# Graph layer on one core: sixty-one groups of edges gathered by other engines instead of sixty, first loads issued earlier, and the last node block's steps in another order

## The chip, the core and the metric

The kernel runs on one core of a Trainium2 chip. A core has five engines that each work through their own list of instructions in order: TensorE (PE; its weight loads are listed apart as PEld), VectorE (DVE), ScalarE (ACT), GpSimd (POOL) and SyncE (SP, which here only issues DMAs). They wait for each other and for DMAs through semaphores. The metric is the device time of one execution in microseconds (us); the time of a kernel is the median of its runs.

## The reference

A message-passing layer over 12,500 nodes (128 features each) and 400,000 edges (32 features each), edges sorted by destination:

```python
h = jnp.maximum(_layernorm(x), 0.0)
m = relu(concat([h[src], h[dst], edge_attr]) @ w1 + b1) @ w2 + b2      # per edge
agg = segment_sum(m, dst)                                               # per node
gi, gh = agg @ w_ih + b_ih, h @ w_hh + b_hh                             # a GRU cell
r, z = sigmoid(i_r + h_r), sigmoid(i_z + h_z)
n = tanh(i_n + r * h_n)
out = x + (1 - z) * n + z * h
```

So each edge needs one row that depends on its source (anywhere in the table), one that depends on its destination (close to that of its neighbours in the list), and its own 32 features.

## The kernel before, in words

**Preamble.** x is read in batches (`load`), normalised, transposed into `hT_all` (features on partitions, all nodes in SBUF), and multiplied by the source part of w1 (table A, in DRAM, stored by the DMAs at line 482) and by the destination part (table B). A loop over `q` holds it; each step of `q` takes four tiles of 128 nodes. The stores of A read a tile `asb` that has two buffers, which ACT fills (line 458). The first nine groups below are gathered from x itself while A is not yet there.

**Groups and units.** The 3,125 tiles of 128 edges make 391 groups `k` of 8 tiles (the first has 5). Half a group is a unit `u`, 782 in all. For each group the program does, in this order along the units: load L (destination numbers and edge features of two groups, `fetch`, lines 566 to 577); load RW, two windows of 32 rows of B (`window_rows`, line 613); turn the destination numbers into a one-hot matrix on DVE (`onehot_T`, line 586); multiply both on PE into PSUM (`pre`, line 683); add the source's rows and clamp at zero (`add` on DVE, line 713); sum by destination on PE with a second one-hot matrix (`seg`, line 739); copy the sums out for every second group (`take`, line 748). In the loop `pre` runs three units ahead of `seg`, `add` two units ahead.

**Where the source's rows come from.** Three ways, fixed before the program is built by the table `mode`:
- by POOL: eight indirect DMAs for a group (line 163), into a ring of `GBUFS` = 11 group buffers. POOL may run ahead of the rest by as many POOL groups as the ring holds.
- by hand on ACT (28 groups) or on DVE (27 groups): the engine copies one column of `hT_all` for each edge into a tile `HE_act` or `HE_dve`, 1,024 small copies for a group on ACT (line 979), 512 double ones on DVE (line 986). PE then multiplies the columns by w1a into the same PSUM tile (line 694) and ACT clamps instead of DVE (line 725).
- by hand on SP (5 groups): one DMA per edge.

The copies of a group by hand are spread evenly over the units since the engine's group before (`jobs`, `run_jobs`), and must be done four units before the group's own. Groups by hand are thus spread over the list: the last ones of ACT, DVE and SP are 388, 386 and 379, and ACT's groups lie 14 or 13 groups apart, which gives its jobs 28 or 26 units each.

**Nodes.** When the groups of a block of nodes are done, `node` runs the GRU cell for that block, one step per unit, on PE, DVE and ACT. The last block (groups 382 to 390) has its own routine, `last_node`, whose steps are called at the units listed in `LAST_STEPS`; what is left of it runs after the loop.

**DMA order.** SP issues nearly all DMAs in program order. The DMAs that are not by hand use eight completion counters by turns (DMAHW0 to DMAHW7 in the rows below); an issue waits until the last DMA of its counter has landed.

Of the kernel before, what the change touches and what calls it, by code (L numbers as in the profile page):

```python
# [9 lines left out]
F32 = mybir.dt.float32  # L10
F16 = mybir.dt.float16
I32 = mybir.dt.int32
U8 = mybir.dt.uint8
# [11 lines left out]
PAIR = 2 * GRP  # L25
# [31 lines left out]
START = {"dve": 14, "act": 4, "sp": 24}  # L57
NR = 12672

H_AT = 16512  # L60
# [3 lines left out]
def tile_gnn(ctx: ExitStack, tc: tile.TileContext, x, src, srcT, dstT, dstP, eaT, eaP, w1, b1, w2T, b2,  # L64
# [126 lines left out]
    base_d = at[96:97, :NP - 1]  # L191
    by_hand = [k for m in ("sp", "act", "dve") for k in order[m]]
    NJ = len(by_hand)
# [109 lines left out]
    def setup(pool):  # L303
# [46 lines left out]
        place(0)  # L350

    st_all = const.tile([128, NT, 2], F32, name="st_all")
    nc.vector.memset(st_all[:, NFULL, :], 0.0)
    with tc.tile_pool(name="pp", bufs=3) as pp:
# [85 lines left out]
        for q in range(NC + 3):  # L440
# [36 lines left out]
            if q in (7, 9, 11):  # L477
                batch_store(q // 2 - 3)
            if q >= 3:
                b, i0, c, e, P, n0 = chunk(q - 3)  # L480
                if e == bats[b][1]:
                    nc.sync.dma_start(nodes(A, i0, e, P), asb[b][:P, :e, :])
# [80 lines left out]

    Ls, OH, RT, HE, SEG = ({} for _ in range(5))
    hand = {}

    def fetch(q):
        if q * QP >= NP:
            return
        n = min(QP, NP - q * QP)  # L570
        c = slice(q * QP * 512, (q * QP + n) * 512)
        Ls[q] = p3.tile([128, QP * 512], F32, name="L")
        p = dstP[:, c]
        nc.sync.dma_start(
            Ls[q].bitcast(I32)[:2 * V, :n * 512],
            bass.AP(tensor=p.tensor, offset=p.offset, ap=[list(p.ap[0]), [0, V], [1, n * 512]]))
        nc.sync.dma_start(Ls[q][2 * V:, :n * 512], eaP[:, c])

# [12 lines left out]

    bases = {}

    def block(k):
        return max(b for b in range(NB) if BLOCKS[b][0] <= k)

    def slot(b, i):
        return i // 2 if b < NB - 1 else (BP - BLOCKS[b][1]) // 2 + i // 2

    def window_rows(k):  # L600
        if k >= NP:
            return
        b = block(k)
        k0, n, _ = BLOCKS[b]
        if k == k0:
            _, vals = nc.values_load_multi_w_load_instructions(
                base_i[0:1, b, 0:n], engines=[ET.SP], min_val=0, max_val=4 * D * LAST,
                skip_runtime_bounds_check_because="clamped above")
            for i, v in enumerate(vals):
                bases[k + i] = v  # L610
        v = bases.pop(k)
        for a in range(2):
            nc.sync.dma_start(RW[k % 4].bitcast(U8)[V * a:V * (a + 1), a, :],
                              B_bytes[bass.ds(v + 4 * D * SHIFT * a, 4 * D * V)].rearrange(
                                  "(p f) -> p f", p=V))

# [144 lines left out]
    def zero(p):  # L761
        nc.tensor.matmul(p, zrow[:, :128], zrow[:, :p.shape[1]], start=True, stop=False)
# [94 lines left out]
    def last_node():  # L857
# [36 lines left out]
        yield  # L894
        ph = gate(two[:, 1, :w], 3, True)
        yield
        for i in (n - 3, n - 2):
# [51 lines left out]
    def one_by_one(m, k):  # L949
        et = {"act": ET.Activation, "dve": ET.DVE, "sp": ET.SP}[m]  # L950
        r = by_hand.index(k)
        if m == "sp":
            goal[k] = tc.alloc_semaphore(f"brought{r}"), 16 * PAIR * 128
            G[k] = pj.tile([128, GRP, 2, D], F32, name="G_sp", bufs=1)
            rows = G[k].bitcast(U8)
        else:
            hand[k] = pj.tile([128, PAIR * 128], F32, name=f"HE_{m}")
# [49 lines left out]
    def run_jobs(u, phase):  # L1007
        if phase == 0:
            for m, k, span in jobs.get(u, ()):
                live[m] = [one_by_one(m, k), u, span, PAIR * 128 // STEP[m], 0]  # L1010
# [20 lines left out]

    gathers(0)
    dst_tile(1)
    for q in range(3):
        fetch(q)
    for k in range(4):
        window_rows(k)

# [33 lines left out]
    last = last_node()  # L1072
    LAST_STEPS = (NU - 8, NU - 6, NU - 5, NU - 4, NU - 3, NU - 2, NU - 1)

# [214 lines left out]
```

## Time and profile before

| | us |
|---|---|
| median of 3 runs (range) | 3378.95 (3376.49 to 3381.35) |
| the profiled execution, as timed | 3383.87 |
| its span, first to last instruction | 3382.1 |
| mean granted TensorE clock | 0.795 |
| busy: PE / DVE / ACT / POOL | 2400.4 / 2213.6 / 3081.1 / 2542.8 |

Busy time leaves out instructions that only load registers or issue DMAs, so an engine can be taken up for longer than it is busy; the page's part on groups of instructions shows such time as idle time that "issue" ended. All times below are us from the start of the span, unless said otherwise. A row of the timeline gives start, length, engine, line, operation, output and input, count, and in brackets the engine's idle time before it and what ended that.

### The profile page before, as it was taken

The numbers are of one execution on the slowest core, as the hardware profiler recorded it, in microseconds if no ns is written. First come the engines' busy times: TensorE is split into PE (matmuls) and PEld (weight loads), VectorE is DVE, ScalarE is ACT, GpSimd is POOL, SyncE is SP. The second block draws the span as 40 slices with busy tenths as digits, with TensorE's granted clock in tenths as the row PEclk, the third lists the DMA queues.
The fourth block names the chain that finished last, engine by engine and source line by source line (L and its number), as shares of the span: only waits on it lengthen the run. The fifth ranks groups of instructions, "written<-read, shape, count | busy, mean of one in ns | idle before, by whom it ended". The sixth has DMA issues, their size and how long they took to land. (4 is left out here: it accounts for less than half of the span.)

```text
span 3382.1 us, 93395 instructions
## 1 busy us (share of the span) xinstructions
PE 2400.4 (71%) x13113; PEld 1554.8 (46%) x13113; DVE 2213.6 (65%) x16274; ACT 3081.1 (91%) x29057; POOL 2542.8 (75%) x2654
## 2 busy tenths in 40 slices
PE   7567766776677677668776777677667767766767
PEld 6444444444444444445444444444444444444445
DVE  8566666766666666666667766666656666666665
ACT  7599899999999998998999999999889998988975
POOL 7777777777777777777777777777777777777775
PEclk9778777887888777877877878787777787778778
DMA  6433444444444444444444444444444444343332
GB/s 215 104 92 84 95 99 101 99 97 103 96 95 99 97 98 95 99 104 97 96 98 97 98 95 105 97 99 98 95 98 96 100 95 99 94 96 94 92 94 67
DMA packets 196737, 335.77 MB, mean 99 GB/s; under 512 B 69445, under 2 KB 118148, under 8 KB 196112
## 3 DMA queue, kind: packets, MB, share of 16 engines
q0 software_dynamic: 84640, 173.51, 23.0%
q1 hardware_dynamic: 111327, 156.18, 17.8%
q14 instruction: 517, 4.23, 0.4%
q8 instruction: 109, 1.79, 0.2%
q10 hardware_dynamic: 144, 0.07, 0.0%
HBM read 309.25 MB, written 20.24 MB: 97 GB/s over the span
## 5 line engine op out<-in xcount | busy, mean ns | idle before, releaser
L163 POOL DMA_INDIRECT G<-A,src_i x2576 | 2475.8, 961 | 790.4 <-issue 761.2
L979 ACT COPY HE_act<-hT_all 128x4 uint8 x28672 | 2889.0, 189 | 52.9 <-issue 29.1
L986 DVE SCALAR_TENSOR_TENSOR both<-hT_all 128x4 uint16 x13824 | 1174.3, 154 | 930.3 <-issue 925.6
L683 PE MATMUL pre<-RW,L 128*128 128x256 f32 x3128 | 1136.1, 489 | 461.3 <-DMA RW<-B 237.7
L683 PEld LDWEIGHTS pre<-RW,L 128*128 128x128 f32 x3128 | 662.8, 237 | 736.8 <-issue 420.2
L739 PE MATMUL seg<-RB,OH 128*32 128x129 f32 x6250 | 592.7, 319 | 244.2 <-DVE RB L713 211.9
L739 PEld LDWEIGHTS seg<-RB,OH 128*32 128x32 f32 x6250 | 328.0, 123 | 590.7 <-DVE RB L713 310.1
L713 DVE CUSTOM_DVE_ANT_0 RB<-pre,G 128x1024 f32<-128x1024 f32 x323 | 391.1, 1211 | 70.9 <-DMA G<-A,src_i 56.5
L586 DVE TENSOR_SCALAR L<-L,node_of 64x512 f32<-64x512 int32 x382 | 185.9, 487 | 62.2 <-DMA L<-in_dstP 59.9
L725 ACT ACTIVATE RB<-pre 128x1024 f32<-128x1024 f32 x64 | 65.0, 1016 | 91.0 <-PE pre L694 91.0
L633 DVE TENSOR_TENSOR OH<-dloc,seg 128x512 f32<-128x512 f16 (+1 forms) x198 | 132.3, 669 | 0.0
L765 PE MATMUL nd<-spot,sums 128*128 128x40 f32 x782 | 119.6, 326 | 3.6 <-DVE sums L748 3.6
L765 PEld LDWEIGHTS nd<-spot,sums 128*128 128x128 f32 x782 | 115.5, 237 | 12.7 <-issue 8.8
L991 DVE COPY HE_dve<-both 128x512 uint8<-128x512 uint8 x216 | 97.6, 452 | 7.4
L244 PE MATMUL nd<-w1b,hT_all 128*128 128x128 f32 x224 | 49.4, 368 | 73.1 <-DVE xb L850 73.1
L734 PE MATMUL seg<-zrow 1*128 1x129 bf16 x196 | 45.5, 232 | 78.1 <-DVE OH L633 78.0
L694 PEld LDWEIGHTS pre<-w1a,HE_dve 128*128 128x128 f32 x432 | 89.1, 255 | 12.4
L694 PEld LDWEIGHTS pre<-w1a,HE_act 128*128 128x128 f32 x448 | 85.9, 238 | 11.0
L694 PE MATMUL pre<-w1a,HE_dve 128*128 128x128 f32 x432 | 85.4, 333 | 0.0
L694 PE MATMUL pre<-w1a,HE_act 128*128 128x128 f32 x448 | 83.7, 319 | 0.0
L163 POOL DMA_INDIRECT G<-in_x,src_i x69 | 65.6, 950 | 21.9 <-issue 20.7
L244 PEld LDWEIGHTS nd<-w1b,hT_all 128*128 128x128 f32 x224 | 35.2, 231 | 85.5 <-DVE xb L850 80.0
(177 smaller groups left out, 1346.2 us busy)
## 6 DMA issues: line engine op xcount, KB each, us to landing
G_sp<-A SPq DMA_DIRECT2D x5120, 0.5 KB
L<-in_dstP SPq DMA_DIRECT2D x195, 256.0 KB
L<-in_eaP SPq DMA_DIRECT2D x195, 256.0 KB
G<-A,src_i POOLq DMA_INDIRECT x2576, 2.5
RW<-B SPq DMA_DIRECT2D x782, 16.0 KB
xb<-in_x SPq DMA_DIRECT2D x26, 256.0 KB
out<-xb SPq DMA_DIRECT2D x26, 256.0 KB
xs<-in_x SPq DMA_DIRECT2D x11, 512.0 KB
```

What stands on the lines that cost most here:

```text
L163: fetched = nc.gpsimd.indirect_dma_start(out=G[k][:, j, a, :], out_offset=None, in_=table, in_offset=bass.IndirectOffsetOnAxis(ap=src_i[c] ...
L244: nc.tensor.matmul(pm[:m, i:i + D], hT_all[:, n0 + i:n0 + i + m], w1b, start=True, stop=True)
L586: nc.vector.tensor_scalar(o, i, node_of[:, k:k + 1], None, op0=ALU.is_equal)
L633: nc.vector.tensor_tensor(p, dloc[:, e0:e1, None].to_broadcast(shape), row[:, None, :].to_broadcast(shape), op=ALU.is_equal)
L683: nc.tensor.matmul(p[:, 2 * i:2 * i + 2, :], Ls[k // QP][:, c0:c0 + 128], RW[k % 4], start=True, stop=not raw)
L694: nc.tensor.matmul(p[:, 2 * i + a, :], cols, w1a, start=False, stop=n + 1 == len(l) or l[n + 1][1] != j)
L713: made = nc.vector._custom_dve(TENSOR_ADD_SAT, out=o, in0=p, in1=G[k].rearrange("p j a f -> p (j a) f")[:, c, :], s0=float("inf"), s1=0.0)
L739: nc.tensor.matmul(p[r0:r0 + V, :D + 1], OH[k][:, a * GRP + j, :], RB[k % 2][:, 2 * j + a, :D + 1], start=False, stop=all(b != a for _, _, ...
L765: nc.tensor.matmul(p[:, bass.ds(offs[i], V + SHIFT)], sums[:, slot(b, i), :D], spot[:, i % 2, :], start=False, stop=i == len(offs) - 1)
L979: nc.scalar.copy(he[:, e * 4:e * 4 + 4], column(v))
L986: nc.vector.scalar_tensor_tensor(both[:, (e0 % PIECE + i) // 2, :], column(vals[i + 1]), 256.0, column(vals[i]), op0=ALU.mult, op1=ALU.add)
L991: nc.vector.tensor_copy(he[:, p0 * 4:(p0 + PIECE) * 4].rearrange("p (n c b) -> p n c b", c=2, b=4), both.bitcast(U8).rearrange("p n (b c) ...
```

## The change

Four things are done.

1. The table `mode` is made anew. Group 385 (`SHARED`) is now by hand as well, the 61st: ACT copies its edges 0 to 767 and DVE 768 to 1023, into one `HE_dve` tile. POOL's list is shorter by that group. The other groups by hand keep their numbers (28, 27, 5) but are placed so that ACT and DVE end at group 385 and SP at 371. ACT's last group of its own is 375, DVE's 381. ACT's groups are now 13 apart in 18 of 27 cases (26 units), 14 in 8 and 12 in one.
2. The first L (`fetch(0)`) is issued at q = 4 of the preamble, over ScalarE's queue instead of SP's, into an `HE_dve` buffer that no one uses yet.
3. The RW rows of groups 0 to 3 are issued at q = 16 of the preamble instead of after the first three L.
4. In `last_node` the degrees start one unit earlier (`LAST_STEPS` now holds NU - 7 too), so each gate comes one unit earlier, and the first six sums of the block, which stood beside the degrees, come in a step of their own behind the gates.

```diff
+SHARED, CUT = NP - 6, 768
...
-    mode, order = {}, {m: [] for m in SPREAD}
+    def share(m, k):
+        return (0, PAIR * 128) if k != SHARED else (0, CUT) if m == "act" else (CUT, PAIR * 128)
+
+    mode, order = {SHARED: "both"}, {m: [] for m in SPREAD}
     for m, n in SPREAD.items():
-        lo, hi = START[m] // 2 + 2, NP - {"dve": 5, "act": 3, "sp": 12}[m]
+        lo, hi = START[m] // 2 + 2, NP - 20
+        part = 0
+        if m != "sp":
+            hi, part = SHARED, (share(m, SHARED)[1] - share(m, SHARED)[0]) / (PAIR * 128)
         for i in range(n):
-            k = lo + int((i + 1) * (hi - lo) / n)
+            k = lo + int((i + 1) * (hi - lo) / (n + part))
...
+        order[m] += [SHARED] if part else []
...
+        if q == 0:
+            Ls[q] = pj.tile([128, QP * 512], F32, name="HE_dve")
+        else:
+            Ls[q] = p3.tile([128, QP * 512], F32, name="L")
         p = dstP[:, c]
+        queue = nc.scalar if q == 0 else nc.sync
...
+            if q == 16:
+                for k in range(4):
+                    window_rows(k)
+            if q == 4:
+                fetch(0)
...
-        pt = ps1.tile([128, 512], F32, name="nd")[:, :w]
-        zero(pt)
-        for i in range(n - 3):
-            sum_of(b, pt, offs, i)
         yield
         carry(b, DEG[0:1, :], pd[0:1, :], d)
...
         ph = gate(two[:, 1, :w], 3, True)
+        yield
+        pt = ps1.tile([128, 512], F32, name="nd")[:, :w]
+        zero(pt)
+        for i in range(n - 3):
+            sum_of(b, pt, offs, i)
...
-        for e0 in range(0, PAIR * 128, LOAD[m]):
+        for e0 in range(*share(m, k), LOAD[m]):
...
+    for q in (1, 2):
+        fetch(q)
     dst_tile(1)
-    for q in range(3):
-        fetch(q)
-    for k in range(4):
-        window_rows(k)
...
-    LAST_STEPS = (NU - 8, NU - 6, NU - 5, NU - 4, NU - 3, NU - 2, NU - 1)
+    LAST_STEPS = tuple(range(NU - 8, NU))
```

How the instructions stand now, at three places. A row is line, operation, output and input, size; the brackets name the counters that it waits for (DMAHW0 to 7 of DMAs, the others of engines). Line numbers of the change are higher by 20 to 48 for the same statement.

ACT's list early in the preamble (seg is a PSUM tile with transposed rows, xs the batch of x), before:

```order
L468 COPY hT_all<-seg_79 128x4x128 [waits PE_49]
L458 COPY asb<-pre 128x512 [waits PE_49]
L263 ACTIVATE xs<-xs,st_all 128x128 [waits DMAHW5_49,DVE_49]
L263 ACTIVATE xs<-xs,st_all 128x128 x3
L458 COPY asb<-pre 128x512 [waits DMAHW5_49,PE_49,Activation_49]
```

and with the change, up to the copy that takes the second `asb` buffer again:

```order
L516 COPY hT_all<-seg_79 128x4x128 [waits PE_49]
L373 DMA HE_dve<-in_dstP 64x1x1024 [waits DMAHW7_49]
L376 DMA HE_dve<-in_eaP 64x1024 [waits DMAHW1_49]
L506 COPY asb<-pre 128x512 [waits PE_49]
L271 ACTIVATE xs<-xs,st_all 128x128 x3
L506 COPY asb<-pre 128x512 [waits DMAHW5_49,PE_49,Activation_49]
L271 ACTIVATE xs<-xs,st_all 128x128 x4
L226 ACTIVATE s<-mv,eps 128x8 [waits DVE_49]
L506 COPY asb<-pre 128x512 [waits DMAHW7_49,PE_49,Activation_49]
```

Two DMA issues stand in ACT's list now, and they use the counters DMAHW7 and DMAHW1; the last copy into `asb` waits for the counter DMAHW7.

SP's list at the same time, the second store of A, before:

```order
L375 DMA xs<-in_x 128x1024 [waits DMAHW1_49,PE_49]
L423 DMA at<-in_src 1x1024 [waits DMAHW2_49]
L423 DMA at<-in_src 1x1024 [waits DMAHW3_49]
L423 DMA at<-in_src 1x1024 [waits DMAHW4_49]
L482 DMA A<-asb 128x1024 [waits DMAHW5_49,Activation_49]
```

and with the change:

```order
L423 DMA xs<-in_x 128x1024 [waits DMAHW3_49,PE_49]
L471 DMA at<-in_src 1x1024 [waits DMAHW4_49]
L471 DMA at<-in_src 1x1024 [waits DMAHW5_49]
L471 DMA at<-in_src 1x1024 [waits DMAHW6_49]
L535 DMA A<-asb 128x1024 [waits DMAHW7_49,Activation_49]
L471 DMA at<-in_src 1x1024 [waits DMAHW0_49]
L471 DMA at<-in_src 1x1024 [waits DMAHW1_49]
```

The second store of A now has the counter whose last DMA is the first half of the early L.

PE's list at the end (seg rows are units 779, 780 and 781; pre<-DEG,brow begins a gate; nd<-spot,sums are sums), before:

```order
L739 MATMUL seg_79<-RB_180,OH_185 32x129 x4
L881 MATMUL pre<-DEG,brow 128x320
L884 MATMUL pre<-hT_all,whh_s 128x320
L734 MATMUL seg_80<-zrow 128x129
L739 MATMUL seg_80<-RB_179,OH_183 32x129 x4
L881 MATMUL pre<-DEG,brow 128x320
L884 MATMUL pre<-hT_all,whh_s 128x320
L739 MATMUL seg_80<-RB_179,OH_183 32x129 x4
L765 MATMUL nd<-spot,sums 128x40
```

and with the change:

```order
L758 MATMUL seg_79<-RB_180,OH_185 32x129 x4
L896 MATMUL pre<-DEG,brow 128x320
L899 MATMUL pre<-hT_all,whh_s 128x320
L753 MATMUL seg_80<-zrow 128x129
L758 MATMUL seg_80<-RB_179,OH_183 32x129 x4
L781 MATMUL nd<-zrow 128x320
L784 MATMUL nd<-spot,sums 128x40
L758 MATMUL seg_80<-RB_179,OH_183 32x129 x4
```

Between the last two units' sums by destination there was a gate; now the first six sums of the block stand there (shown by their first two rows).

More of the change, by code (lines that the diff above doesn't have):

```diff
@@ L350, in setup, with fetch, block, window_rows @@
         place(0)
+    Ls = {}
+    def fetch(q):
+        if q * QP >= NP:
+            return
+        n = min(QP, NP - q * QP)
+        c = slice(q * QP * 512, (q * QP + n) * 512)
+        if q == 0:
+            Ls[q] = pj.tile([128, QP * 512], F32, name="HE_dve")
+        else:
+            Ls[q] = p3.tile([128, QP * 512], F32, name="L")
+        p = dstP[:, c]
+        queue = nc.scalar if q == 0 else nc.sync
+        queue.dma_start(
+            Ls[q].bitcast(I32)[:2 * V, :n * 512],
+            bass.AP(tensor=p.tensor, offset=p.offset, ap=[list(p.ap[0]), [0, V], [1, n * 512]]))
+        queue.dma_start(Ls[q][2 * V:, :n * 512], eaP[:, c])
+    bases = {}
+    def block(k):
+        return max(b for b in range(NB) if BLOCKS[b][0] <= k)
+    def window_rows(k):
+        if k >= NP:
+            return
+        b = block(k)
+        k0, n, _ = BLOCKS[b]
+        if k == k0:
+            _, vals = nc.values_load_multi_w_load_instructions(
+                base_i[0:1, b, 0:n], engines=[ET.SP], min_val=0, max_val=4 * D * LAST,
+                skip_runtime_bounds_check_because="clamped above")
+            for i, v in enumerate(vals):
+                bases[k + i] = v
+        v = bases.pop(k)
+        for a in range(2):
+            nc.sync.dma_start(RW[k % 4].bitcast(U8)[V * a:V * (a + 1), a, :],
+                              B_bytes[bass.ds(v + 4 * D * SHIFT * a, 4 * D * V)].rearrange(
+                                  "(p f) -> p f", p=V))
     st_all = const.tile([128, NT, 2], F32, name="st_all")
@@ L561, in check_windows @@
         nc.vector.tensor_copy(flag, f[:, 6:7])
-    Ls, OH, RT, HE, SEG = ({} for _ in range(5))
+    OH, RT, HE, SEG = ({} for _ in range(4))
     hand = {}
[L567 to L577, printed above, removed]
     def onehot_T(k):
```

27 lines of the change are left out of this document (5 added, 22 removed).

## The prediction

> **What bounds the kernel now.** I read the page's busy times and groups first, then the gathers (line 163) and the additions (line 713) counted over stretches from the start, then the timeline of both ends, then the by-hand copies of ACT (line 979) job by job.
>
> ```profile
> PE 2400.4 (71%) x13113; PEld 1554.8 (46%) x13113; DVE 2213.6 (65%) x16274; ACT 3081.1 (91%) x29057; POOL 2542.8 (75%) x2654
> L163 POOL DMA_INDIRECT G<-A,src_i x2576 | 2475.8, 961 | 790.4 <-issue 761.2
> L979 ACT COPY HE_act<-hT_all 128x4 uint8 x28672 | 2889.0, 189 | 52.9 <-issue 29.1
> ```
>
> ACT is the busiest by the page. But POOL's gathers with the idle time ahead of each fill 2475.8 + 790.4 = 3266.2 us, and 761.2 of the idle time is "issue": no one else holds POOL up. One gather costs 3266.2 / 2576 = 1.268 us. Whether POOL or the rest ends last is told by their distance. Line 163 from 0 to 300, 2300 and 3300 us (stretch, busy time and count, clock, DMA share, GB/s), then line 713 in the same stretches:
>
> ```profile
> 0.00:300.00 300.00, 221.02 (x233) 0.84 0.47 128
> 0.00:2300.00 2300.00, 1739.77 (x1811) 0.80 0.42 102
> 0.00:3300.00 3300.00, 2498.89 (x2601) 0.79 0.42 100
> ```
>
> ```profile
> 0.00:300.00 300.00, 12.13 (x10) 0.84 0.47 128
> 0.00:2300.00 2300.00, 265.75 (x219) 0.80 0.42 102
> 0.00:3300.00 3300.00, 387.37 (x319) 0.79 0.42 100
> ```
>
> A group is eight gathers (the first five), so POOL has gathered (233 - 5) / 8 + 1 = 29.5 groups at 300 us, 226.8 at 2300, 325.5 at 3300. Consumed are the additions, plus nine groups from x that need none, less those of SP's groups (0, 3, 4): 19, 225, 324. POOL leads by 10.5 groups, then 1.8, then 1.5: the consumers start far behind, are faster, and have caught up by 2300. From there POOL sets the pace, and its last gather sets the end:
>
> ```profile
> 3344.34 1.02 ACT L725 ACTIVATE RB<-pre 128x1024 f32<-128x1024 f32 x1
> 3344.98 0.95 POOL L163 DMA_INDIRECT G<-A,src_i  x1 [0.30 <-issue]
> 3354.97 0.94 POOL L163 DMA_INDIRECT G<-A,src_i  x1 [0.30 <-issue]
> DMA to landing us min/median/max: 2.5/2.5/2.5
> 3356.16 1.22 DVE L713 CUSTOM_DVE_ANT_0 RB<-pre,G 128x1024 f32<-128x1024 f32 x1 [1.50 <-PE pre L683]
> 3356.87 1.53 PE L765 MATMUL nd<-spot,sums 128*128 128x40 f32 x12
> 3361.10 1.29 DVE L713 CUSTOM_DVE_ANT_0 RB<-pre,G 128x512 f32<-128x512 f32 x2 [3.15 <-PE pre L683]
> 3365.12 0.63 PE L739 MATMUL seg<-RB,OH 128*32 128x129 f32 x8
> 3365.69 0.80 PE L881 MATMUL pre<-DEG,brow 34*128 34x320 f32 x2
> 3367.16 0.63 PE L739 MATMUL seg<-RB,OH 128*32 128x129 f32 x8
> ```
>
> The last gather lands at 3354.97 + 2.5 = 3357.5, and the span ends at 3382.1: a tail of 24.6. A part of it is a late consumer: group 389 landed at 3344.98 + 2.5 = 3347.5 and was added at 3356.16, 8.7 later; group 390 was added 3.6 after landing, behind PE.
>
> **Group 385 leaves POOL.** Eight gathers by 1.268: -10.1 us. Both ends: 9.99 between the last gathers of groups 389 and 390, so eight cost 10.0 to 10.1.
>
> **The first loads.** The start, by the timeline:
>
> ```profile
> 90.21 0.66 SPq L574 DMA_DIRECT2D L<-in_dstP  x1
> 92.84 0.94 POOL L163 DMA_INDIRECT G<-A,src_i  x1 [3.18 <-DMA L<-in_dstP]
> 100.32 0.48 DVE L586 TENSOR_SCALAR L<-L,node_of 64x512 f32<-64x512 int32 x1 [9.76 <-DMA L<-in_dstP]
> 106.01 0.66 PE L666 MATMUL misc<-ident,G 128*128 128x128 f32 x2 [13.77 <-ACT G L263]
> 118.39 1.19 PE L683 MATMUL pre<-RW,L 128*128 128x256 f32 x2 [11.73 <-DMA RW<-B]
> 124.86 0.94 POOL L163 DMA_INDIRECT G<-A,src_i  x1 [2.34 <-PE misc L666]
> ```
>
> The first product waited 9.76 us for L and then 11.73 for RW. With both loads early, both waits go: 21.5 us sooner. By itself this is worth nothing at the end, because POOL, not the consumers, is last there; it is margin for ACT (below). But one wait of POOL goes with it: at 124.86 it stood 2.34 us instead of 0.30 for the transposes at line 666, which now come well ahead. -2.0 us.
>
> **What the early L costs.** It takes DMA counters in the middle of A's stores, and the second store of A now waits until the early L has landed.
>
> ```profile
> 20.00:30.00 10.00, 9.40 (x50) 8.87 (x48) 7.76 (x40) 9.15 (x22) 7.57 (x9) 1.00 0.83 263
> 25.51 0.63 ACT L458 COPY asb<-pre 128x512 f32<-128x512 f32 x1
> 26.56 0.37 SPq L482 DMA_DIRECT2D A<-asb  x1
> 33.95 0.59 ACT L458 COPY asb<-pre 128x512 f32<-128x512 f32 x1 [0.26 <-ACT xs L263]
> 86.31 3.37 SPq L482 DMA_DIRECT2D A<-asb  x3
> ```
>
> Bounds: if L lands before SP comes to that store, nothing. At most it takes as long as later, 90.21 to its use at 100.32, 10.1 us: issued at about 25.7 it lands by 35.8, and the store leaves then and not at 26.56. A store took some 3.4 us (the last three, issued from 86.31 on, let POOL go at 92.84, 89.68 + 3.2), so ACT's copy at 33.95, which needs that buffer back, would start at 39.3, 5.4 late, and SP's next loads stand behind the store as well. Every engine is 76 to 94% taken in that stretch, so little is made up, and A is finished later by 0 to 6 us. I take +4, nearer the upper end, because L is 512 KB in a stretch in which the DMA engines are already 83% taken. POOL's first gather from A comes at 96.8 then, and everything behind it 4 us later. The Trainium skill ("DMA: Bandwidth & Descriptors", "Issuing engines are not separate DMA queues") says that transfers issued by several engines share the same 16 DMA engines, so that a second issuer saves issue time only. It speaks against this part, and by it alone the early L would put off the rest by its bytes, an estimate of 0.524 MB / 263 GB/s = 2.0 us; the term would be +2.0 and the time 2 us shorter. No run here shows the two apart. The RW rows are 8 small DMAs of SP at q = 16; they lie beside the same stores and I cost them at nothing of their own (0 to 2 us if SP's stores are late through them, in the range).
>
> The last gather lands at 3357.5 - 10.1 - 2.0 + 4 = 3349.4.
>
> **The end.** By hand, ACT now ends four units ahead of group 385, at unit 766, and groups 386 to 390 all come from POOL, at 10 us each. At the end of before ACT still copied for group 388, and its clamp at 3344.34 was followed by the last addition of 390 at 3361.10, nine units later: 16.8 / 9 = 1.87 us per unit once the copies are gone, against 5 that POOL takes. So the consumers wait for POOL at the last groups. From the landing, the first of 390's additions (0.65, half of 1.29) and the hand-over (0.15) lead to the sum by destination of unit 780 at 3350.2, where before it was at 3365.12; the rest was 3382.1 - 3365.12 = 17.0. In it six first sums with their zeroing (0.23 + 1.53) now stand where a gate stood (3365.69 to 3367.16, 1.47): +0.3. The last gate stays behind unit 781. 3350.2 + 17.0 + 0.3 = **3367.5**, or -14.6 against 3382.1. The profiled execution took 3383.87, 4.92 more than the median, and the difference is taken over to that: 3378.95 - 14.6 = 3364.
>
> **Whether ACT keeps up.** This is the step on which the sum hangs: ACT gets 0.75 groups more, and its jobs mostly 26 units instead of 28. A job (1,024 copies; line 979 from its first copy to the next job's first: stretch, ACT's busy time and count) does not depend on its units, but on what it waits for:
>
> ```profile
> 142.60:263.80 121.20, 102.34 (x1025) 0.77 0.38 91
> 489.20:602.30 113.10, 102.73 (x1026) 0.79 0.42 99
> ...
> sum 558.80, ACT 515.35; mean ACT 103.07
> ```
>
> ```profile
> 602.30:710.50 108.20, 102.36 (x1024) 0.82 0.42 98
> ...
> sum 655.50, ACT 618.02; mean ACT 103.00
> ```
>
> ```profile
> 710.50:823.80 113.30, 102.39 (x1025) 0.80 0.42 98
> ...
> sum 804.50, ACT 720.22; mean ACT 102.89
> ```
>
> The first row is the first job. Up to 2300, where ACT is not held by POOL, the five jobs of 26 units took 558.8 / 5 = 111.8 us, the six of 28 units right behind them 109.25, the seven later ones 114.9. With 28 units ACT runs ahead and waits for the others; behind a 26 it has fallen back and hardly waits. Now 18 jobs have 26 units and no two of 28 follow each other, so I expect 109.25 for most, and at the worst (8 x 109.25 + 19 x 111.8) / 27 = 111.0. The first job starts 142.6 - 17.5 (21.5 less the 4) = 125.1 and ends 121.2 later, at 246.3; 27.75 jobs more end at 3278 to 3327; twelve units by 1.87 bring the last addition to 3300 to 3349. The landing at 3349.4 is later than either, so POOL still ends last, at the worst by nothing. A price per job of 111.0 is thus the point from which ACT decides. DVE (27.25 groups for 27) and SP (its 5 groups ending sooner) get only 1 to 2% more per unit, against 5% for ACT; should DVE decide instead, that is the same rival (B) by another engine.
>
> **Rivals.** (A) The consumers stay late at the end, so that the tail keeps its 24.6: 3349.4 + 24.6 = 3374.0, median 3371. For it: 389 was 8.7 us behind. Against it: POOL needs 50 us for five groups that cost the consumers 19. Chance 0.13. (B) The other side: ACT becomes the bound. Its place is the jobs of 26 units: if they go on costing the mean of the 18 jobs, (558.8 + 655.5 + 804.5) / 18 = 112.2, then 246.3 + 27.75 x 112.2 = 3360, the last addition at 3382, and some 18 behind it 3400: median 3397, +18. For it: the margin is thin and ACT is 91% busy. Against it: the jobs behind a 26. Chance 0.20. (C) The preamble loses the whole gain: SP's list, which also feeds x, stalls behind the store twice over, 10 us and more instead of 4: the span becomes 3367.5 + 6 to 8 = 3373.5 to 3375.5, the median 3370 to 3372. For it: the 83% of the DMA engines. Against it: the trace has only one store that meets the early L. Chance 0.09.
>
> **How the numbers follow.** The forecast has the remaining 0.58. A measurement of this kernel can tell about 0.2%, 6.8 us, from no change: faster lies below 3372.2, slower above 3385.7. The forecast's own range is 3357 (L costs nothing, and 3 us less of tail) to 3371. Faster: nearly all of the 0.58, most of (A), and what of (C) lies below the bound: 0.68. Slower is (B) but for its mild form just past the point: 0.19. Within: 0.13. The range for eight in ten goes up to 3388, which holds A, C and a mild B.
>
> **What would show it.** POOL issues 2568 gathers from A, the first at about 96 and the last near 3347; no stop of 2.3 us near 125; ACT's copy into `asb` at 34 waits for a DMA (if not, the +4 is wrong); the first clamp of ACT at 109 instead of 126.86 as in this row of before:
>
> ```profile
> 126.86 1.00 ACT L725 ACTIVATE RB<-pre 128x1024 f32<-128x1024 f32 x1
> ```
>
> Line 979's jobs at 109 to 111 us; the additions of 389 and 390 within 4 us of landing. If the additions still trail POOL by two groups at 2300 us and later, with ACT's copies up to unit 766 ending after 3330, (B) holds and the forecast is wrong.

## The result, and the profile after

The changed kernel takes 3391.64 us (median of 8 runs, 3385.58 to 3395.3), the kernel before 3380.59 (8 runs beside them): a ratio of 1.0033, with a 95% interval of 1.0023 to 1.0043. It is slower by 11 us, where 3364 was forecast. The profiled execution of the change took 3386.99, its span is 3385.1 us, 3.0 longer than that of before.

POOL did what it was to do. The last two of its rows and, from the same timeline, the last addition on DVE:

```profile
3340.23 0.94 POOL L171 DMA_INDIRECT G<-A,src_i  x1 [0.30 <-issue]
3341.47 0.94 POOL L171 DMA_INDIRECT G<-A,src_i  x1 [0.31 <-issue]
...
3363.15 1.29 DVE L732 CUSTOM_DVE_ANT_0 RB<-pre,G 128x512 f32<-128x512 f32 x2 [3.46 <-PE pre L702]
```

POOL's last gather starts at 3341.47 instead of 3354.97, 13.5 us sooner. But it lands at about 3344, and the last addition comes 19 us behind that; in before it was 3.6. The consumers, not POOL, now set the end. The gathers (line 171) and the additions (line 732) of the change, counted from 0 to 300, 2300 and 3300 us, in the form in which they were shown of before:

```profile
0.00:300.00 300.00, 216.98 (x228) 0.83 0.47 129
0.00:2300.00 2300.00, 1733.82 (x1812) 0.80 0.42 101
0.00:3300.00 3300.00, 2492.25 (x2603) 0.80 0.42 100
```

```profile
0.00:300.00 300.00, 13.42 (x12) 0.83 0.47 129
0.00:2300.00 2300.00, 260.55 (x215) 0.80 0.42 101
0.00:3300.00 3300.00, 384.19 (x317) 0.80 0.42 100
```

By the same working POOL has gathered 28.9, 226.9 and 325.8 groups, and the consumers have used 12 + 9 = 21, 215 + 9 - 3 = 221 and 317 + 9 - 5 = 321. The lead is 7.9 groups at 300 us (before 10.5, the earlier start is seen in it), but still 5.9 at 2300 (before 1.8) and 4.8 at 3300 (before 2.5: five of SP's groups had been added by then, the last at 3289, not the four of the prediction). The consumers never catch POOL up. By the counts of PE's products of line 702 (683 in before; 8 for a group) between 300 and 2000 us, before and then the change:

```profile
300.00:2000.00 1700.00, 599.70 (x1652) 0.80 0.42 98
```

```profile
300.00:2000.00 1700.00, 594.58 (x1632) 0.80 0.42 97
```

206.5 groups have become 204.0; a group takes 8.33 us instead of 8.23. The page and the start of the change:

```profile
L171 POOL DMA_INDIRECT G<-A,src_i x2568 | 2459.0, 958 | 793.8 <-issue 766.5
...
L702 PE MATMUL pre<-RW,L 128*128 128x256 f32 x3112 | 1140.2, 493 | 447.1 <-DMA RW<-B 288.5
```

```profile
22.80 1.15 ACTq L373 DMA_DIRECT2D HE_dve<-in_dstP  x1
...
36.35 0.37 SPq L535 DMA_DIRECT2D A<-asb  x1
...
39.64 0.58 ACT L506 COPY asb<-pre 128x512 f32<-128x512 f32 x1 [6.02 <-DMA A<-asb]
...
100.46 0.94 POOL L171 DMA_INDIRECT G<-A,src_i  x1 [10.83 <-DMA L<-in_dstP]
...
114.22 1.00 ACT L744 ACTIVATE RB<-pre 128x1024 f32<-128x1024 f32 x1
```

The early L held back the second store of A until 36.35 (26.56 before), ACT's copy waited 6.02 us behind it, and POOL's first gather from A came at 100.46 instead of 92.84: 7.6 us late. Not all of that is the early L's, as the section on the prediction shows. The first clamp came at 114.22 instead of 126.86, 12.6 sooner, where 109 had been forecast.

### The profile page after: what moved, and what is told of

The parts are those of the page before. It is cut to its first block, busy times and chain, and to the rows that moved or that the text cites. A ratio compares the mean times of both kernels' runs of the same rounds, so it can differ in the third digit from the quotient of the medians.

```text
span 3385.1 us, 94355 instructions
## 1 busy us (share of the span) xinstructions
PE 2399.5 (71%) x13129; PEld 1538.9 (45%) x13129; DVE 2221.3 (66%) x16403; ACT 3165.9 (94%) x29826; POOL 2526.0 (75%) x2646
## 5 line engine op out<-in xcount | busy, mean ns | idle before, releaser
L171 POOL DMA_INDIRECT G<-A,src_i x2568 | 2459.0, 958 | 793.8 <-issue 766.5
L784 PE MATMUL nd<-spot,sums 128*128 128x40 f32 x782 | 104.3, 301 | 1.3 <-DVE sums L767 1.3
L784 PEld LDWEIGHTS nd<-spot,sums 128*128 128x128 f32 x782 | 100.3, 210 | 9.2 <-issue 7.5
L833 PE MATMUL nd<-DEG,brow 34*128 34x512 f32 (+2 forms) x112 | 69.8, 706 | 29.8 <-ACT gt L843 29.5
L713 PEld LDWEIGHTS pre<-w1a,HE_dve 128*128 128x128 f32 x448 | 78.7, 219 | 9.3
L1000 ACT COPY HE_dve<-hT_all 128x4 uint8 x768 | 77.1, 189 | 1.5 <-issue 0.8
L713 PE MATMUL pre<-w1a,HE_dve 128*128 128x128 f32 x448 | 76.9, 300 | 0.0
```

What stands on the lines that cost most here:

```text
L171: fetched = nc.gpsimd.indirect_dma_start(out=G[k][:, j, a, :], out_offset=None, in_=table, in_offset=bass.IndirectOffsetOnAxis(ap=src_i[c] ...
L713: nc.tensor.matmul(p[:, 2 * i + a, :], cols, w1a, start=False, stop=n + 1 == len(l) or l[n + 1][1] != j)
L784: nc.tensor.matmul(p[:, bass.ds(offs[i], V + SHIFT)], sums[:, slot(b, i), :D], spot[:, i % 2, :], start=False, stop=i == len(offs) - 1)
L833: nc.tensor.matmul(pg, brow[:, c], DEG[:, :w], start=True, stop=False)
L1000: nc.scalar.copy(he[:, e * 4:e * 4 + 4], column(v))
```

## The experiments

Four theories were tried. **T**: the consumers set the end, and of them ACT's copies alone set the pace. **R1**: POOL still sets the end, and its late start on A ate the gain. **T2**: ACT and DVE together set the pace. **T3**: SP sets it, because the rows of B (RW), which PE needs for each product, stand on SP's queue behind the row loads of SP's own groups. Each ratio is to the kernel before, run beside the version. There before takes 3379.3 to 3382.5 us, but about 5700 beside six of the runs, which the last part of this section is about.

**Which parts cost or bring something: e1b, e3b, f1, f2.** e1b has the table of before, e3b the first L on SP behind the preamble, f1 and f2 are one kernel with both.

```diff
e1b, f1, f2:
-    mode, order = {SHARED: "both"}, {m: [] for m in SPREAD}
+    mode, order = {}, {m: [] for m in SPREAD}
-        lo, hi = START[m] // 2 + 2, NP - 20
+        lo, hi, part = START[m] // 2 + 2, NP - {"dve": 5, "act": 3, "sp": 12}[m], 0
e3b, f1, f2:
-            if q == 4:
-                fetch(0)
...
-    for q in (1, 2):
+    for q in range(3):
         fetch(q)
```

> The table of before (60 groups) with the early first L, the early rows of B and the last block's new order; again, on a chip on which before takes about 3380. Theory T: the consumers catch POOL up before 2400 and POOL, which starts on A 7.6 us later, sets the end: 3380.6 + 7.6 - 2 - up to 3 = 3383 to 3386. Rival R1 (POOL sets the end in the change too): 3391.6 + 10 = 3402.

Measured: 3385.56 us, 1.0019 (1.001 to 1.0028), as T had it; R1's 3402 is out.

> The first L back on SP behind the preamble, all else as in the change; again, on a chip on which before takes about 3380. POOL's first gather from A at 92 to 94 instead of 100.5. Theory T (consumers set the end): as the change or up to 3 us more, 3391 to 3394. Rival R1 (POOL sets the end): 7.6 us less, 3384.

Measured: 3392.7 us, 1.0041 (1.0027 to 1.0054), the time of the change, though POOL starts on A at 95 instead of 100.5. So POOL's start does not set the end of the change; R1 falls. The consumers' start does not show in the time either: PE's first product comes at 118.39 in before, at 111.00 in e3b and at 105.39 in the change, 7.4 us sooner by the early rows of B and 5.6 more by the early L.

> The table of before (60 groups by hand), the first L on SP behind the preamble as before, the early rows of B and the last block's new order kept: the change without its 61st group and without its early L. Theory T: POOL sets the end as in before; its first gather from A is at 92 to 94 again, the wait of 2 us near 125 is gone, and the consumers start 11 us sooner: 2 us faster than before, 3376 to 3381 on a chip on which before takes 3380.6. Rival R1 (POOL's start alone counts): 3378 too. Rival R2 (the consumers' pace sets the end in before as well): 11 us faster, 3370.

> The version without the 61st group and the early L (table of before, early rows of B, new order of the last block), now timed. All theories: POOL sets the end; the wait of 2 us near 125 is gone, so 1 to 3 us faster than before, 3376 to 3379; if the last block's new order is worth anything it shows here as more than that.

Measured: f1 3381.53 beside 3382.47 (one run each), f2 3379.97, 0.9997 (0.9988 to 1.0006). Without the 61st group and the early L the change is worth nothing that can be measured; the 1 to 3 us expected of f2 do not show. e1b and f2 differ by the early L: e1b is 6.2 us above its before, f2 0.6 below its own, 6.8 apart. POOL's first gather from A is at 100.42 in e1b and at 94.09 in f2, 6.3 apart. Where POOL sets the end, the early L is a loss of that size.

**ACT or DVE: e2b, g1, h1, h2.** e2b gives DVE 256 of ACT's edges of the shared group; h1 lets DVE load 16 column numbers at a time. g1 is e2b and e3b together, h2 is g1 and h1.

```diff
e2b, g1, h2:
-SHARED, CUT = NP - 6, 768
+SHARED, CUT = NP - 6, 512
h1, h2:
-LOAD = {"act": 16, "dve": 32, "sp": 32}
+LOAD = {"act": 16, "dve": 16, "sp": 32}
```

> Group 385 cut in half between ACT and DVE (ACT 512 of its edges instead of 768), all else as in the change; again, on a chip on which before takes about 3380. Theory T (ACT's copies set the consumers' pace, and the consumers the end): 256 copies fewer on ACT, 27 us, so the consumers end up to 27 us sooner, down to where POOL's landing at 3345 and a tail of 20 set the end: 3365 to 3375. Rival R2 (DVE sets the pace): a quarter of a group more on DVE, 28 us: 3405 to 3420. Rival R1 (POOL): no change, 3391.

> A version put together from the parts: 61 groups with group 385 cut in half, the first L back on SP behind the preamble, early rows of B, the new order of the last block. Theory T: POOL's last gather lands at about 3345 - 7.6 = 3338, the consumers' last addition comes where e2b has it; the later one and 20 us of tail set the end: 3362 to 3372, the same as e2b where the consumers decide. Rival R2 (DVE sets the pace): 3405 to 3420. Rival R1: 3384.

Measured: e2b 3400.07, 1.0051 (1.0037 to 1.0065); g1 3398.85, 1.0051 (1.0037 to 1.0064). By the medians they are 8 and 7 us slower than the change; the intervals overlap with its own, so that this much is not certain, but they are not faster by 20. ACT's 27 whole jobs, of 1,024 copies in both, took 112.7 us each in e2b, where its groups lie a little farther apart, and 110.8 in the change. So it is not the number of its copies that sets ACT's pace, and T in this form falls; but R2's 28 us are not there either. The places moved by more than the one group that was expected (ACT's last own group from 375 to 379, DVE's from 381 to 378), and both shares of group 385 end late, ACT's at 3348.9 and DVE's at 3348.0, against 3327.9 and 3330.4 in the change:

```profile
3317.82 31.08 ACT L1000 COPY HE_dve<-hT_all 128x4 uint8 x307
...
3347.57 0.43 DVE L1012 COPY HE_dve<-both 128x512 uint8<-128x512 uint8 x1
```

The clamp of group 385 cannot come before that. What makes the shares late, and whether it is all of the 8 us, was not tried.

> The change with DVE loading its column numbers 16 at a time instead of 32; the copies and all else stay. In the change DVE stands 955 us ahead of its copies with 'issue' as the reason, 1.1 us for each of 872 loads of 32; a load of 32 takes 2.15 us on its queue, one of ACT's 16 takes 1.05. Theory T2 (ACT and DVE share the blame: each waits for the other, and both are full): the standing time falls by a third or more, DVE comes free, ACT's full jobs go from 110.8 to 108 or 109, the consumers end 40 us or more sooner, POOL's landing at 3345 sets the end: 3366 to 3378. Theory T (ACT alone): ACT's jobs stay at 110 to 111, no change, 3388 to 3394. If loads of 16 hide no better than those of 32, DVE stands longer, 2 x 1 us for 32: the jobs get longer and the time goes up by 20 or more, which again speaks for DVE as part of the bound.

> As the run before with loads of 16, and group 385 cut in half (ACT 512), and the first L back on SP behind the preamble. If loads of 16 help, theory T2: both engines end sooner, POOL lands at 3339 and sets the end: 3358 to 3368. Theory T: ACT is relieved by 27 us, DVE no matter: 3365 to 3375. If loads of 16 hurt: 3410 or more.

Measured: h1 3383.76, 1.0022 (1.0012 to 1.0032); h2 3386.18, 1.0024 (1.0011 to 1.0037). The row of DVE's copies in h1:

```profile
L1007 DVE SCALAR_TENSOR_TENSOR both<-hT_all 128x4 uint16 x13952 | 1227.8, 156 | 862.8 <-issue 848.3 <-DMA RW<-B 2.1 <-DMA L<-in_eaP 1.6
```

DVE stood 863 us instead of 955, a tenth less and not a third, so the run was a weak test. The groups went no faster: between 300 and 2000 us they were 203.0 against 204.0, and the last addition came at 3361.6 against 3363.15. Both times lie between the ranges that were given. By the median h1 is 8 us faster than the change, by the ratios 4, and the intervals overlap. That DVE has no part is not shown by it; i2 below is the stronger test.

**One engine at a time: i1, i2, i3.** Each leaves out a quarter of one engine's by-hand work in its own groups; for ACT:

```diff
+        if m == "act" and k != SHARED:
+            return 0, 768
         return (0, PAIR * 128) if k != SHARED else (0, CUT) if m == "act" else (CUT, PAIR * 128)
...
+        if m == "act" and k != SHARED:
+            nc.scalar.copy(hand[k][:, 768:1024], hT_all[:, 0:256])
         for e0 in range(*share(m, k), LOAD[m]):
```

> The change, but in each of ACT's 28 own groups only 768 of 1024 columns are copied one by one; the last 256 come as one block of wrong columns, so part of the sum is wrong. ACT loses a quarter of its work, some 25 us a job; places and all else stay. Theory T (ACT alone sets the consumers' pace, 8.35 us a group between groups 30 and 230): the pace falls to where the next engine stands, 7.9 or less, the consumers catch POOL up, and POOL's landing at 3345 with a tail of 20 sets the end: 3364 to 3372. Theory T2 (ACT and DVE, each waiting for the other): the pace falls to 8.1 or 8.2 only, the end is still POOL's: 3364 to 3375. Theory T3 (ACT and SP, whose row loads PE waits for): the same 8.1 or 8.2.

> The change, but in each of DVE's 27 own groups only 768 of 1024 columns are copied one by one, the last 256 as one wrong block. DVE loses a quarter of its by-hand work. Theory T (ACT alone): no change, pace 8.35, 3388 to 3394. Theory T2 (ACT and DVE): ACT's jobs fall from 110.8 to 108 or 109, pace 8.2, 3366 to 3380. Theory T3 (ACT and SP): pace 8.3 to 8.35, 3384 to 3394.

> The change, but in each of SP's 5 groups only 768 of 1024 rows are fetched one by one; the last 256 come as two DMAs of 128 wrong rows each. SP loses a quarter of its by-hand issues, some 80 us of issuing a group. Theory T3 (SP is late with the rows of B, RW, for which PE stood 230 us between 600 and 3200 in the change): those waits fall by half or more, ACT's jobs go to 108 or 109, pace 8.2, 3366 to 3380. Theory T (ACT alone) and T2 (ACT and DVE): pace 8.35 as in the change, 3388 to 3394.

Measured: i1 3372.58, 0.9975 (0.9965 to 0.9984); i2 3372.75, 0.9974 (0.9964 to 0.9983); i3 3370.08, 0.9971 (0.9958 to 0.9984). By the times alone all three engines are to blame: each relief is enough to bring the last addition back to POOL's landing. The time of i2 lies 11 us below what T3 gave for it, so T3 alone does not explain the end. How the reliefs work is told by three views between 300 and 2000 us: the count of PE's products (8 a group), PE's waits there for RW (sum, times, longest), and the row loads of SP's second group (duration on the queue, start of the first and of the last). The change; its row of products is shown above:

```profile
PE pre L702 <- DMA RW<-B: 201.4, 53, 9.7
L989 SPq DMA_DIRECT2D G_sp<-A x1024: 224/228/431, 849.1 to 1408.7; - x171
```

i1, a quarter less on ACT:

```profile
300.00:2000.00 1700.00, 590.27 (x1624) 0.80 0.42 98
PE pre L704 <- DMA RW<-B: 323.7, 71, 9.0
L993 SPq DMA_DIRECT2D G_sp<-A x1023: 224/228/520, 832.0 to 1389.4; - x171
```

i2, a quarter less on DVE:

```profile
300.00:2000.00 1700.00, 596.97 (x1621) 0.79 0.42 97
PE pre L704 <- DMA RW<-B: 382.5, 81, 11.9
L993 SPq DMA_DIRECT2D G_sp<-A x1024: 224/228/874, 850.3 to 1410.9; - x171
```

i3, a quarter less on SP:

```profile
300.00:2000.00 1700.00, 598.74 (x1672) 0.80 0.42 99
PE pre L704 <- DMA RW<-B: 9.4, 2, 5.5
L998 SPq DMA_DIRECT2D G_sp<-A x768: 224/228/532, 834.2 to 1367.3; - x192
```

With less on ACT or on DVE the groups go no faster in this stretch (203.0 and 202.6 of them against 204.0), and PE's waits for RW grow from 201 us to 324 and 383: the engine that was relieved now waits for SP, through PE. SP's group takes its 557 to 561 us in all three, whatever the others do. With less on SP the waits for RW are gone, 9 us, and 209.0 groups are done. So SP sets the pace in the long middle of the change. T and T2 fall for the middle, T3 stands: its time and its pace for i3 came (ACT's jobs at 109.6 us, a little above its 108 to 109), while the faster pace that all three gave for i1 did not.

That is not so at both ends. The products of line 758 (the sums by destination, 16 a group; lines 739, 760 and 753 in the other versions), counted from the start to four times:

| | 300 us | 2000 us | 2900 us | 3330 us |
|---|---|---|---|---|
| before | 314 | 3618 | 5354 | 6130 |
| the change | 330 | 3594 | 5306 | 6114 |
| i1, less on ACT | 366 | 3610 | 5362 | 6194 |
| i2, less on DVE | 346 | 3594 | 5330 | 6176 |
| i3, less on SP | 330 | 3674 | 5362 | 6218 |
| j1b (below) | 328 | 3658 | 5362 | 6194 |

Between 300 and 2000 us the change falls behind before, by 40 products or 2.5 groups, and only less load on SP makes that good. i1 and i2 win groups before 300 us, have lost most or all of that lead again by 2000, and gain after it: i2 has 62 products, 3.9 groups, more than the change at 3330 and none more at 2000. In those stretches ACT and DVE have a part. Which of them holds the other there was not taken apart.

The new table raised SP's load. Its groups had been 87, 160, 233, 306 and 379 and are now 85, 156, 228, 299 and 371; the 1,024 row loads of the second group are spread over 132 units instead of 136 (SP starts two units behind its group before, and must be done eight units ahead of its own). In before they run from 868.9 to 1433.3, and PE waits for RW there as well, between 300 and 2000 us:

```profile
PE pre L683 <- DMA RW<-B: 200.9, 55, 9.4
L968 SPq DMA_DIRECT2D G_sp<-A x1024: 224/228/684, 868.9 to 1433.3; - x171
```

564.4 / 136 = 4.15 us a unit, against 559.6 / 132 = 4.24 in the change: 2.2% more per unit, and the pace of the whole is 8.33 / 8.23, 1.2% worse over a stretch that also holds the pauses between SP's groups. PE's waits for RW are the same 201 us in both kernels, so the waits do not tell before and the change apart. It fits that SP was full in before already, and that the new table put more on it and on ACT.

**The load of SP with all rows loaded: j1b.** The first L as in e3b, and SP's five groups spread from unit 12 to group 383 (84, 158, 233, 309, 383).

```diff
-START = {"dve": 14, "act": 4, "sp": 24}
+START = {"dve": 14, "act": 4, "sp": 12}
-        lo, hi = START[m] // 2 + 2, NP - 20
+        lo, hi = START[m] // 2 + 2, NP - 8
```

> The version with SP's five groups spread from unit 12 to group 383 and the first L on SP behind the preamble, again, on a chip on which before takes about 3380. It differs from e3b (3392.7) in the places of SP's groups alone. Theory T3 (SP's row loads hold up RW, PE and so all consumers): pace between groups 30 and 230 falls from 8.31 (e3b) to 8.2 or less, PE's waits for RW shrink, the consumers' last addition moves from 3359 to near POOL's landing: 3362 to 3376. Theory T (ACT's copies alone): as e3b, 3388 to 3396.

Measured: 3361.81 us, 0.9947 (0.9933 to 0.996): faster than before by 19 us and than e3b, from which it differs by SP's places only, by 31. The same three views, then the last gather and the last addition; the first row is e3b's (the profiled executions took 3382.1 and 3367.1):

```profile
PE pre L697 <- DMA RW<-B: 224.3, 55, 9.5
...
300.00:2000.00 1700.00, 596.79 (x1668) 0.80 0.42 98
PE pre L697 <- DMA RW<-B: 55.9, 12, 8.6
L984 SPq DMA_DIRECT2D G_sp<-A x1024: 224/228/647, 825.8 to 1394.0; - x171
```

```profile
3344.40 0.94 POOL L171 DMA_INDIRECT G<-A,src_i  x1 [0.30 <-DMA G<-A,src_i]
3347.06 0.69 DVE L727 CUSTOM_DVE_ANT_0 RB<-pre,G 128x512 f32<-128x512 f32 x1 [4.33 <-DMA G<-A,src_i]
```

SP takes 568.2 / 138 = 4.12 us a unit, the waits for RW are 56 us instead of 224 in e3b, 208.5 groups are done, and the last addition waits for the gather's landing: POOL sets the end again, with a 61st group by hand and the same number of copies on ACT and DVE as in the change. ACT's jobs of 26 units are no obstacle to that. This is the version that beats both kernels. Its load on SP for a unit is below that of before too (five groups over 706 units; 686 in before, 670 in the change). So j1b shows that the load on SP alone makes the difference between a loss and a gain; how much of the loss comes back with just the load of before it does not show.

**Runs beside which before takes 5700 us: e1, e2, e3, e4, j0, j1.** Beside these six, four of them versions that were also run at 3380, before takes 5708 us (5692 for the last two). The first four ran on the chip that the record numbers 4, the last two on number 15, and e1b, e2b, e3b and g1 had run on number 15 as well, 50 minutes earlier, beside a before of 3379. So it is not shown that the chip makes the difference. The granted clock is 0.66 to 0.67 instead of 0.80. ACT's idle time is ended by "issue"; the row of its copies in e1, where before had 29.1 us of "issue":

```profile
L997 ACT COPY HE_act<-hT_all 128x4 uint8 x28672 | 3160.8, 189 | 2174.7 <-issue 2147.4
```

DVE's copies have 1675.8 us of "issue" there, where before had 925.6. With its idle time ACT's copies fill 3160.8 + 2174.7 = 5335.5 of 5709.6 us, so that ACT is probably the bound; no run tests it. The parts are worth something else then: e1 (60 groups) 0.9997 (0.9979 to 1.0015), e2 (512 edges on ACT) 1.014 (1.0111 to 1.017), e3 (768) 1.021 (1.0182 to 1.0239), and j1, which as j1b gains 0.5%, 1.0221 (1.02 to 1.0243). Two kernels ran at this speed only. e4 has the last block's steps in the order of before; j0 is the change with SP's last group at 379.

```diff
e4:
-    LAST_STEPS = tuple(range(NU - 8, NU))
+    LAST_STEPS = (NU - 8, NU - 6, NU - 5, NU - 4, NU - 3, NU - 2, NU - 1)
j0:
-        lo, hi = START[m] // 2 + 2, NP - 20
+        lo, hi = START[m] // 2 + 2, NP - 12
```

> The change with the table of before (60 groups by hand, none shared); the early first loads and the last block's new order stay. Theory T (the consumers set the end of the changed kernel: ACT's jobs of 110.8 us up to unit 766 at 3328.0, then PE without a gap; POOL's last gather at 3342 has 18 us to spare): with 60 groups the consumers run at about 8.19 us a group again, catch POOL up before 2300, and POOL sets the end. POOL starts on A at 100.5 as in the changed kernel, 7.6 later than before, less 2 for the wait near 125: 3380.6 + 5.6 = 3386, 3381 to 3387. Rival R1 (POOL still sets the end, and its late start on A ate the gain): eight gathers more than in the changed kernel, 3391.6 + 10 = 3402.

> The change with group 385 cut in half: ACT copies its edges 0 to 511 instead of 0 to 767, DVE the rest; the other groups move by one place at most. Theory T (ACT's copies set the consumers' pace): ACT has 256 copies less, about 27 us at 0.106 us each, and the consumers end up to 27 us sooner, until POOL's landing at 3345 and a tail of 20 set the end: 3365 to 3372. Rival R2 (DVE sets the pace of the units, ACT only follows): DVE gets a quarter of a group more, 28 us: 3405 to 3420. Rival R1 (POOL): no change, 3391.

> The change with the first L back on SP behind the preamble, into its own buffer; the early rows of B, the 61st group and the last block's order stay. All theories: POOL's first gather from A is back at 92 to 94 (100.5 in the change) and ACT's copy into asb near 34 waits no more. The first product then waits for L but not for RW, and comes at 107 against about 106. Theory T (consumers set the end): same time as the change, 3391 to 3394. Rival R1 (POOL sets the end): 7.6 us faster, 3384.

> The change with the last block's degrees, gates and sums in the order of before; all else stays. Theory T: PE has no gap from 3328 on, the same products stand there in another order, so the time moves by no more than the 1.8 us by which six sums and the zeroing displace a gate of 1.5: 3389 to 3394. Rival R4 (the new order is what costs): 5 us or more faster, under 3387.

> The change with SP's five groups spread up to group 379 as in before (87, 161, 233, 306, 379) instead of up to 371; ACT's and DVE's places move by one group at most, the 61st group and all else stay. Theory T3 (SP's row loads hold up the rows of B, RW, and so PE and all consumers): SP's work for a unit falls by 2 to 3%, the pace between groups 30 and 230 from 8.35 to about 8.25, the consumers end some 20 us sooner: 3372 to 3384. Theory T (ACT's copies alone): pace 8.35, no change, 3388 to 3394.

> As j0, but SP's five groups are spread wider still, from unit 12 instead of 24 and up to group 383 (84, 158, 233, 309, 383), and the first L is back on SP behind the preamble. Theory T3: SP's work for a unit falls by 5 to 6% against the change, pace 8.2 or less, POOL's last gather lands at 3340 and sets the end or nearly: 3362 to 3374, faster than both kernels. Theory T: 3388 to 3394.

Measured: e4 1.0202 (1.0175 to 1.0228), j0 1.0202 (1.0183 to 1.0222), neither apart from e3. These runs test none of the numbers in the expectations, which are worked out for a before of 3380. So what the last block's order does by itself at 3390 us stays open; f2, which has it, shows that it and the early rows of B bring nothing together. Open too is j0, which would have set SP's load back to that of before and no further.

## Why the prediction was wrong

**Group 385 leaves POOL, and POOL's wait near 125.** Right. POOL issued 2568 gathers from A, and stood nowhere near 125.

**What the early L costs.** The mechanism was right, and its size was taken too small: +4, where the traces show 5.1 to 6.3, about the upper bound of 6. POOL's first gather from A comes at 100.46 in the change and at 95.35 in e3b, which lacks the early L; at 100.42 in e1b and 94.09 in f2. The rest of the 7.6 us is there without the early L: with the early rows of B alone the first gather comes 0.6 to 2.5 us behind the 92.84 of before (f1, j1b, f2, e3b, one trace each). The sum had these rows at nothing, the range at 0 to 2.

The bound rested on L landing within 10.1 us of its issue, as later in the program; issued at 22.80, its first half let the store go at 36.35, 13.5 us on. The trace names SP's wait for it:

```profile
SPq L535 <- DMA HE_dve<-in_dstP: 9.9, 1, 9.9
```

The 2.0 us estimated by the bytes from the rule of the Trainium skill ("DMA: Bandwidth & Descriptors", "Issuing engines are not separate DMA queues") fall short of the 5.1 to 6.3. The wait in the trace is for a counter, which the rule does not speak of, and no run here shows what sharing the DMA engines costs.

**POOL's end.** With 7.6 for the early L and the early rows together the sum would have put the last gather at 3354.97 - 10.1 - 2.0 + 7.6 = 3350.5; it started at 3341.47. The gathers from A took, without the first one's wait, (2459.0 + 793.8 - 10.83) / 2568 = 1.262 us each instead of 1.266 in before ((3266.2 - 3.18 - 2.04) / 2576). That makes 9 us over the list. Why they were quicker was not tried.

**Whether ACT keeps up: the step that failed.** Its price for a job held by the number. From the first to the last whole job of ACT in the change:

```profile
252.10:3243.10 2991.00, 2795.77 (x27649) 0.79 0.42 97
```

27 jobs at 2991 / 27 = 110.8 us, inside the 109.25 to 111.0 that were given, though at its worse end. With SP relieved the same jobs took 2960.2 / 27 = 109.6 us in i3 and 2958.8 / 27 = 109.6 in j1b, near the 109.25 that was expected of most. Over 27.75 jobs the 1.2 us make 33.

So the step failed first in asking only ACT, because ACT's load for a unit rose most, 5% against 1 to 2% for SP and DVE; SP's part was put at nothing. By the table it rose by 2.4% (five groups over 670 units instead of 686). But a small rise counts in full on an engine that has no slack, and that SP had little was to be suspected from before, where the first row of PE's waits is for the rows of B, which stand on SP's queue (sum, times, longest):

```profile
PE pre L683 <- DMA RW<-B: 237.7, 66, 11.7
```

i1 to i3 and j1b show that SP's row loads, through RW and PE, set the pace of the middle and with it ACT's waits. Rival (B) named the right outcome with the wrong engine; its price, ACT's jobs at 112.2, did not come.

Second, the way from ACT's last copy to the last addition was 12 units at 1.87 us, 22. It took from 3328.0 (252.1 + 2991 + 84.8 for the shared part) to 3363.15, 35 us. PE had no gap in that stretch (stretch, then busy time and count of PE, PEld, DVE, ACT and POOL):

```profile
3328.00:3363.00 35.00, 35.00 (x228) 22.70 (x227) 18.71 (x49) 2.37 (x4) 11.06 (x12) 0.95 0.24 63
```

The 1.87 was read from a stretch of before (3344.3 to 3361.1) in which PE has no product of a gate; at 3328 PE still had the gates of the block before between the units, some 8 us of products at lines 833 to 837. With the start 6 us later than taken (252.1 for 246.3 at the end of the first job) and this 13 us, the last addition comes 14 us behind the landing that was forecast, and 19 behind the one that came. With jobs at 109.6 us ACT would have been done some 33 us sooner, an estimate from the two prices; in j1b, which starts later by 2, its last copy ended at 3301.5, 26 us sooner, and POOL was last. The margin of the worst case had been "nothing", and a chance of 0.20 for the other side was too small for that.

**The end.** Where the consumers are in time, the tail is as forecast: in j1b from the last gather's landing at 3346.9 to the span's end at 3365.3 it is 18.4 us, against 3367.5 - 3349.4 = 18.1. Rival (A) is refuted there. Its 3361.8 is also near the 3364 that the sum gave for a change whose consumers keep up, but that is in part luck, for the terms are others: no early L, and gathers that took longer.

## What to carry to other kernels

When work is moved between engines that run in step, the question is not which load rises most but which engine has no slack: a queue that only issues DMAs can be that engine, and its busy share is not in the page. What is in the page is who waits for its DMAs: here the first row of PE's waits already pointed at it. Relieve one engine at a time and look at whom the others then wait for. Reliefs that give the same time can do it in different stretches, and counts and waits by stretch tell them apart where the times do not.

## What the runs showed of the hardware that was not expected

A DMA of 256 KB, the first half of the early L, let go of its counter 13.5 us after its issue, in a stretch in which the DMA engines are 80% taken (20 to 30 us of the change). SP stood 9.9 us for it, with everything behind it in its queue. The same half, issued at 90.21 in before, where they are 62% taken (90 to 100 us), was in use 10.1 us later.

1,024 DMAs of one row each took SP 557 to 564 us in before, the change, i1 and i2, 0.55 us a row, though a row shows only 0.23 us on the queue. A quarter less by-hand work on ACT (i1) or on DVE (i2) did not change that.

The same program took 5700 us instead of 3380 beside six of the runs. ACT's single-column copies stood 2147 us for "issue" there and DVE's 1676, while one copy of ACT took the same 189 ns; the granted clock was 0.67. Why is not shown. A table of work that is balanced at one of these speeds is not at the other: j1b is 0.5% faster than before at 3380, j1, the same kernel, 2.2% slower at 5700.

Halving the size of DVE's register loads (16 numbers for 32, so twice as many) took only a tenth off the time that DVE stands for them, 955 to 863 us.
